# Two graph layers on one core: the first layer's result is kept in the output tensor, and the output stage's DMA adds the second layer's to it

## The chip, the cores and the metric

The kernel runs on one core of a Trainium2 chip. The core has five engines that run side by side, each with its own queue of instructions: TensorE (PE; its weight loads are listed apart as PEld), VectorE (DVE), ScalarE (ACT), GpSimd (POOL) and SyncE (SP). Data moves between the chip's memory and the on-chip SBUF through 16 DMA engines; here SP and POOL issue all transfers. TensorE writes its results to PSUM, from where VectorE or ScalarE copies them on. The metric is the time of one execution in microseconds of device time, as the median of several runs.

## What is computed

Sixteen graphs of 1024 nodes and 256 channels pass through two layers that share one adjacency matrix. The reference, cut to what matters here:

```python
# x: (16, 1024, 256), adj: (1024, 1024)
h = maximum(layernorm(x), 0)
x = x + layer0(h, para, adj, kv_w)          # attention over the nodes, weighted graph product as query
h = maximum(layernorm(x), 0)
x = x + layer1(h, adj, W1, b1, g1, be1, W2, b2, g2, be2)
return x

# layer1, in short
agg = A_hat @ h                             # A_hat: adj + I, scaled by the degrees
z   = relu(batchnorm(agg @ W1.T + b1))      # mean and variance over all graphs and nodes
y   = z @ W2.T + b2
out = batchnorm(y)                          # again over all graphs and nodes
```

Two things set the shape of the program. Each batch norm needs the statistics of all 16 graphs before any graph can go on. And the last line adds the second layer's output to `x` as it was after the first layer (called x1 here), so x1, 16 MB in all, has to be kept until the end.

## The kernel before

The batch is `B = 16`, the nodes are tiled in `NT = 8` tiles of `P = 128`, the channels in `CC = 2` chunks of 128. The function `layers` holds the first phase (layer 0, and of layer 1 everything up to `agg @ W1.T`), the function `second` holds the rest. `layers(False)` is what the profile shows. A second pass, `layers(True)`, stands behind a condition on a value that the kernel computes; no instruction of it appears in the profile. The order of the instructions on each engine is written out by hand (`tc.manual_schedule`), so what the program says in order is issued in that order.

**First phase.** Attention runs graph after graph, four scores and values steps at a time, and between these steps the generator `background(b)` supplies the other products: keys, values and queries of the next graph, the aggregate and the hidden product of the graph before. When graph b's attention is complete, `normed(b)` (line 780) takes the second layer norm of `xs[b]`, the tile that now holds x1. Then POOL stores that tile to a scratch tensor in DRAM, `x1_d[b]` (line 784; for the last graph line 795), in which each of the 128 partitions has its 8 KB in one piece. SP reloads the same SBUF tile with the input of graph b + 3 (`load_x`, line 173) and must wait for the store to have read it. Behind that load in SP's queue stand the loads of `aht`, the pieces of the combined adjacency matrix that the aggregate multiplies with (line 687, always five pieces ahead).

**Second phase, products.** `second` first runs the products `z @ W2.T` for all graphs (`graph(b, ahead)`, line 1319), reads the hidden values `yin` back from DRAM on SP's queue (line 1270), and keeps `y2[b]`, channels on partitions, in SBUF. At five places between the graphs, and before the output stage, it calls `load_x1` (line 1229). This function picks a buffer `xo` for the next graph, out of eleven in turn (three of their own, four of `yin`'s, one of `both`, and three of graphs whose `y2` is used up), and issues two loads of 512 KB from `x1_d` on SP's queue, one for each half of the nodes.

**Output stage** (from line 1430). When the statistics are complete, for each graph:

- ScalarE scales and shifts `y2[b]` in place, one instruction of 128x1024 for each of the two channel chunks (line 1437; for graph 0 four of 128x512);
- TensorE turns it, 128x128 at a time, into PSUM tiles `pt` of two node tiles each: 16 transposes in four groups of four, in four PSUM banks (line 1445);
- VectorE adds each group to its quarter of `xo` (line 1451);
- after two groups POOL stores that half, 512 KB, to `out` (line 1452), four node tiles of 1 KB rows for each partition;
- then `load_x1` fetches the next graph's x1, once its buffer is free.

The compiler gives POOL's transfers eight semaphores in turn, so a store waits until the eighth one before it has landed.

Of the kernel before, what the change touches and what calls it, by code (L numbers as in the profile page):

```python
# [10 lines left out]
F32 = mybir.dt.float32  # L11
AF = mybir.ActivationFunctionType
ALU = mybir.AluOpType
# [4 lines left out]
P = 128  # L18
# [5 lines left out]
def gnn_two_layers_kernel(  # L24
# [12 lines left out]
    nc = tc.nc  # L37
    B, N, C = x.shape
    H1 = w1_t.shape[1]
    NT = N // P  # L40
# [12 lines left out]
    dram = ctx.enter_context(tc.tile_pool(name="dram", bufs=1, space=DRAM))  # L53
# [9 lines left out]
    stats1 = const.tile([P, HC, B * NH, 6], F32, name="stats1")  # L63
    mv1 = const.tile([P, HC, 2], F32, name="mv1")

    x1_d = [dram.tile([P, NT, C], F32, name=f"x1_d{b}") for b in range(B)]


    aht_d = dram.tile([7, NP // 2, P, TH, FB], F32, name="aht_d")
# [27 lines left out]
    def layers(shifted):  # L97
# [22 lines left out]
        xs, hs, hts, ats, qs, ks, vs = {}, {}, {}, {}, {}, {}, {}  # L120
# [20 lines left out]
        def run(*parts):  # L141
            for part in parts:
                while advance(part) is not None:
                    pass
            while queue:
                queue.pop(0)()

        def weave(main, *sides):

            for i, cost in enumerate(main):  # L150
                for start, side in sides:
                    if i >= start:
                        cost += next(side, 0.0)
                yield cost
            for _, side in sides:
                yield from side
# [16 lines left out]
        def load_x(b):  # L173
            xs[b] = p3.tile([P, NT, C], F32, tag="x", name=f"x_{b}")
            for half in range(2):
                t = slice(half * NT // 2, (half + 1) * NT // 2)
                nc.sync.dma_start(
                    out=xs[b][:, t], in_=x[b].rearrange("(t p) c -> p t c", p=P)[:, t]
                )
# [205 lines left out]
        def transposed(b, k, halves=range(NH)):  # L385

            h = hs["a", b]
            if 0 in halves:
                ht = p3.tile([P, N], F32, tag="ht", name=f"ht_{b}_{k}")
                hts.setdefault(b, []).append(ht)  # L390
            ht = hts[b][k]
            for g in halves:
                pt = bank(f"htp_{b}_{k}_{g}")
                for j in range(FB // P):
                    t = g * (FB // P) + j
                    nc.tensor.transpose(
                        pt[:, j * P : (j + 1) * P], h[:, t, k * P : (k + 1) * P], ident
                    )
                nc.scalar.copy(ht[:, g * FB : (g + 1) * FB], pt)  # L399
# [351 lines left out]
        def hidden(b):  # L751
# [7 lines left out]
            for n, (g, j) in enumerate(parts):  # L759
# [17 lines left out]
                    soon(lambda: next(turns[0]))  # L777
                yield 1.71

        def normed(b):  # L780
            while (b, NH - 1) not in complete:
                yield 0.1
            yield from Norm(b, False).all()
            nc.gpsimd.dma_start(out=x1_d[b], in_=xs[b])
            if b + 3 < B:
                load_x(b + 3)

        def normed_last():

            norm = Norm(B - 1, False)  # L790
            for half in range(NH):
                while (B - 1, half) not in complete:
                    yield 0.0
                yield from norm.half(half * NT // 2)
            nc.gpsimd.dma_start(out=x1_d[B - 1], in_=xs[B - 1])

        def summed(b):
            yield from Norm(b, True).all()
# [346 lines left out]
        with st:  # L1145
            if shifted:
                for b in range(B):
                    if b > 0:
                        load_x(b)
                    run(Norm(b, True).all())  # L1150
                    differences(b)
                    for k in range(CC):
                        transposed(b, k)
                    run(islice(weighers[b], AHEAD))
                    run(weave(plain_queries(b), (0, weighers[b])))
                    if b == 0:
                        run(degrees(), graph())
                        load_later()
                    run(keys_values(b))
                    shifted_attention(b)  # L1160
                    norm = Norm(b, False)
                    run(norm.all())
                    nc.gpsimd.dma_start(out=x1_d[b], in_=xs[b])
                    if b == B - 1:
                        attn.close()
                        turns.append(second(kind))
                    run(aggregate(b), hidden(b))
            else:
                norm = Norm(0, True)
                norm.stats(0, 1)  # L1170
                norm.scale(0, 2)
                for t in range(2, NT, 2):
                    norm.stats(t, t + 1)
                    norm.shift(t - 2, 2)
                    norm.relu(t - 2, t - 1)
                    norm.scale(t, 2)
                norm.shift(NT - 2, 2)
                norm.relu(NT - 2, NT - 1)
                products = keys_values(0)

                for k in range(CC):
                    transposed(0, k, (0,))
                run(islice(products, 2))
                for k in range(CC):
                    transposed(0, k, (1,))
                differences(0)
                run(weave(products, (0, islice(weighers[0], AHEAD))))
                load_x(1)
                load_x(2)
                run(weave(plain_queries(0), (0, weighers[0]), (5, Norm(1, True).all())))  # L1190
                attention()
                attn.close()
                turns.append(second(kind))
                run(aggregate(B - 1), hidden(B - 1))
# [3 lines left out]
    def second(kind):  # L1198
# [27 lines left out]

        xos = []

        def load_x1():


            b = len(xos)
            name = f"xo_{kind}_{b}"
            HT = NT // 2
            if not 8 <= b < 11:
                pool, tag = ((xp, "xo"), (io, "yin"), (wp, "both"))[(b % 11 > 2) + (b % 11 > 6)]
                xo = pool.tile([P, NT, C], F32, tag=tag, name=name)
                halves = [xo[:, :HT, :], xo[:, HT:, :]]
            else:
                halves = [  # L1240
                    yp.tile([P, HT, C], F32, tag=f"y2_{b - 8}_{i}", name=f"{name}_{i}")
                    for i in range(2)
                ]
            for i in range(2):
                nc.sync.dma_start(out=halves[i], in_=x1_d[b][:, i * HT : (i + 1) * HT, :])
            xos.append(halves)

        with st:
# [165 lines left out]
            xp = st.enter_context(tc.tile_pool(name=f"xp_{kind}", bufs=3))  # L1414
            for b in range(B):
                graph(b, ahead_of(b + 1))
                if b in (1, 3, 5, B - 2, B - 1):
                    for _ in range(1 + b // (B - 2)):
                        load_x1()
                if kind == "f" and b == B // 2:  # L1420
                    look()
                if kind == "f" and b == B // 2 + 2:
                    flag(ps.tile([P, FB], F32, tag="pz", name=f"good_{kind}")[:, 0:1])

            scales(1)
            for _, finish, _ in affs:
                finish()
            while len(xos) < min(8, B):
                load_x1()
            for b in range(B):  # L1430

                for part in range(2 if b == 0 else 1):
                    n = slice(part * FB, N if b > 0 else (part + 1) * FB)
                    for k in range(CC):
                        s2, sh2 = affs[k][2]
                        y = y2[b][k][:, n]
                        nc.scalar.activation(y, y, AF.Identity, bias=sh2, scale=s2)
                for half in range(2):
                    xo = xos[b][half]
                    for g in range(NT // 4):  # L1440
                        pt = ps.tile([P, 2, C], F32, tag="pz", name=f"pt_{kind}_{b}_{half}_{g}")
                        for j in range(2):
                            t = half * NT // 2 + 2 * g + j
                            for k in range(CC):
                                nc.tensor.transpose(
                                    pt[:, j, k * P : (k + 1) * P],
                                    y2[b][k][:, t * P : (t + 1) * P],
                                    ident,
                                )
                        dst = xo[:, 2 * g : 2 * g + 2, :]  # L1450
                        nc.vector.tensor_add(dst, pt, dst)  # L1451
                    nc.gpsimd.dma_start(  # L1452
                        out=out[b].rearrange("(h t p) c -> h p t c", h=2, p=P)[half], in_=xo
                    )
                if len(xos) < B:
                    load_x1()

    fp = ctx.enter_context(tc.tile_pool(name="fp", bufs=1))
    bad = fp.tile([1, 1], mybir.dt.int32, name="bad")
# [16 lines left out]
    with tc.manual_schedule():  # L1476
        layers(False)
# [41 lines left out]
```

## Time and profile before

| | |
|---|---|
| median of 3 runs | 2539.81 us (2537.09 to 2540.54) |
| the profiled execution: time | 2539.22 us |
| the profiled execution: span of its instructions | 2537.4 us |
| mean granted TensorE clock | 0.986 |
| TensorE busy | 2443.6 us (96%) |
| VectorE, ScalarE, POOL busy | 74%, 55%, 17% |
| DMA traffic | 424 MB, mean 167 GB/s |
| first activation of the output stage | 2461.28 us |
| last `out` store issued | 2524.26 us |

How to read it. The span is the time from the first to the last instruction of one profiled execution, and all positions in the text are microseconds from its start. A group's line gives engine, operation, output and inputs by the program's names, shapes and count, then the busy time in all, the mean of one in ns, the idle time of the engine just before these instructions, and what ended that idle time. "L1451" is line 1451 of the kernel. The granted clock is the share of full speed that the chip's throttle let TensorE have. A DMA's landing time runs from its issue to its completion. The busy share over the whole span hides the stages: the output stage is only the last 76 us of 2537.4.

### The profile page before, as it was taken

The numbers are of one execution on the slowest core, as the hardware profiler recorded it, in microseconds if no ns is written. First come the engines' busy times: TensorE is split into PE (matmuls) and PEld (weight loads), VectorE is DVE, ScalarE is ACT, GpSimd is POOL, SyncE is SP. The second block draws the span as 40 slices with busy tenths as digits, with TensorE's granted clock in tenths as the row PEclk, the third lists the DMA queues.
The fourth block names the chain that finished last, engine by engine and source line by source line (L and its number), as shares of the span: only waits on it lengthen the run. The fifth ranks groups of instructions, "written<-read, shape, count | busy, mean of one in ns | idle before, by whom it ended". The sixth has DMA issues, their size and how long they took to land. (4 is left out here: it accounts for less than half of the span.)

```text
span 2537.4 us, 35520 instructions
## 1 busy us (share of the span) xinstructions
PE 2443.6 (96%) x13343; PEld 833.1 (33%) x13343; DVE 1886.3 (74%) x2924; ACT 1399.2 (55%) x1919; POOL 428.8 (17%) x532
## 2 busy tenths in 40 slices
PE   8979999999999999999999999999999999999994
PEld 3323333333333333333333333333333332234443
DVE  4658787777878687878777787868786866656774
ACT  6756464747474655646474747465565634345553
POOL 1460101010101101010101010110101001036653
PEclk9989999999999999999999999999999999999997
DMA  4663535444454535352544444443535244355459
GB/s 141 202 213 97 218 97 198 136 178 162 170 166 146 183 131 181 102 204 89 207 131 177 159 170 166 172 157 133 184 112 195 84 154 160 131 216 216 182 200 363
DMA packets 189108, 424.03 MB, mean 167 GB/s; under 512 B 22200, under 2 KB 84672, under 8 KB 181120
## 3 DMA queue, kind: packets, MB, share of 16 engines
q1 hardware_dynamic: 161408, 312.87, 36.4%
q0 software_dynamic: 27520, 108.81, 11.3%
q8 instruction: 107, 1.75, 0.3%
q14 instruction: 73, 0.60, 0.1%
HBM read 316.94 MB, written 104.66 MB: 166 GB/s over the span
## 5 line engine op out<-in xcount | busy, mean ns | idle before, releaser
L931 ACT ACTIVATE p<-sc 128x1024 f32<-128x1024 f32 x512 | 495.0, 1019 | 637.0 <-PE sc L923 636.6
L953 DVE TENSOR_TENSOR acc<-acc,p 128x1024 f32<-128x1024 f32 x384 | 470.9, 1226 | 172.4 <-ACT p L931 151.8
L923 PE MATMUL sc<-q,k 64*64 64x512 f32 x4096 | 503.3, 607 | 8.8 <-ACT p L931 8.8
L964 PE MATMUL o<-p,v 128*64 128x512 f32 x2048 | 497.2, 606 | 2.2 <-DVE os L978 2.2
L171 PE MATMUL pg<-w,h_a 128*64 128x512 f32 x1600 | 359.8, 592 | 0.9 <-DVE w L467 0.9
L171 PE MATMUL pa<-aht,h_b 128*64 128x512 f32 x1536 | 347.4, 594 | 5.5 <-DMA aht<-aht_d 4.9
L480 ACT ACTIVATE w<-cbc,csum 128x512 f32<-128x512 f32 x256 | 285.8, 1168 | 0.0
L923 PEld LDWEIGHTS sc<-q,k 64*64 64x64 f32 x4096 | 132.0, 133 | 354.1 <-issue 300.9
L467 DVE SCALAR_TENSOR_TENSOR w<-w,adj 128x1024 f32<-128x1024 f32 x128 | 156.3, 1221 | 111.6 <-ACT w L488 91.5
L171 PE MATMUL py<-at,w 128*64 128x512 f32 x1024 | 229.2, 594 | 0.0
L982 POOL DMA_DIRECT2D out_d<-os x63 | 35.6, 565 | 1126.7 <-DVE os L978 1121.4
L964 PEld LDWEIGHTS o<-p,v 128*64 128x64 f32 x2048 | 125.2, 137 | 305.2 <-issue 274.4
L171 PEld LDWEIGHTS pg<-w,h_a 128*64 128x64 f32 x1600 | 114.8, 137 | 229.1 <-issue 219.2
L171 PEld LDWEIGHTS pa<-aht,h_b 128*64 128x64 f32 x1536 | 110.3, 137 | 220.0 <-issue 201.8
L767 ACT ACTIVATE y<-py,vec 128x512 f32<-128x512 f32 x128 | 87.4, 683 | 120.6 <-PE py L171 97.0
L488 ACT ACTIVATE w<-w 128x1024 f32<-128x1024 f32 x128 | 135.1, 1056 | 1.7
L542 DVE TENSOR_TENSOR w<-w,w 128x1024 f32<-128x1024 f32 x112 | 132.7, 1215 | 1.5
L768 POOL DMA_DIRECT2D y_d<-y x128 | 69.3, 541 | 350.3 <-ACT y L767 345.5
L171 PEld LDWEIGHTS py<-at,w 128*64 128x64 f32 x1024 | 74.4, 138 | 146.1 <-issue 133.3
L171 PE MATMUL pk<-ht,kvw_f 128*64 128x512 f32 x512 | 117.6, 603 | 1.5 <-ACT ht L399 1.5
L171 PE MATMUL pv<-kvw_f,ht 128*64 128x256 f32 x1024 | 116.1, 379 | 0.0
L950 DVE TENSOR_TENSOR acc<-p,p 128x1024 f32<-128x1024 f32 x64 | 78.7, 1230 | 49.8 <-ACT p L931 49.7
(163 smaller groups left out, 2639.2 us busy)
## 6 DMA issues: line engine op xcount, KB each, us to landing
aht<-aht_d SPq DMA_DIRECT2D x224, 512.0 KB, 6.5
adj<-in_adj_dram SPq DMA_DIRECT2D x128, 512.0 KB, 4.7
y_d<-y POOLq DMA_DIRECT2D x128, 256.0 KB, 4.0
yin_f<-y_d SPq DMA_DIRECT2D x32, 1024.0 KB, 6.4
x<-in_x_dram SPq DMA_DIRECT2D x32, 512.0 KB, 5.3
para<-in_para_dram SPq DMA_DIRECT2D x64, 256.0 KB, 3.1
x_d<-x POOLq DMA_DIRECT2D x16, 1024.0 KB, 9.9
xo_f<-x_d SPq DMA_DIRECT2D x32, 512.0 KB, 8.1
```

The lines of the kernel that those rows point to most:

```text
L171: nc.tensor.matmul(dst[r], left[:, r], right, start=start, stop=stop)
L467: nc.vector.scalar_tensor_tensor(w, w, 1.0, a, op0=ALU.add, op1=ALU.mult)
L480: nc.scalar.activation(w[:, t, :].rearrange("p (t q) -> p t q", q=P), cbc[:, q * NT // NH : (q + 1) * NT // NH], AF.Abs, bias=csum[:, th * ...
L488: nc.scalar.activation(made[i], made[i], AF.Tanh, scale=-0.5 / C)
L542: nc.vector.tensor_sub(block(i)[part], block(x)[part], block(y)[part])
L767: nc.scalar.activation(y, made, AF.Identity, bias=b1[:, j : j + 1])
L768: nc.gpsimd.dma_start(out=y1_d[i][:, j, :], in_=y)
L923: nc.tensor.matmul(sc[part, e, :], ks[b][k][r, m * P + c * HW : m * P + (c + 1) * HW], qs[b][k][r, f * FB : (f + 1) * FB], start=True, sto ...
L931: nc.scalar.activation(pr, sc, AF.Exp)
L950: nc.vector.tensor_add(self.acc, self.held, pr)
L953: nc.vector.tensor_add(self.acc, self.acc, pr)
L964: nc.tensor.matmul(self.o[r, :], vs[b][k][:, m, r], pr[:, e, :], start=(m == 0), stop=(m == NT - 1),)
```

## The change

x1 is no longer stored to `x1_d`, which goes away. A new function `keep(b)` stores it to `out[b]`, in the output's layout. It is called where the stores to `x1_d` stood. `load_x1` becomes `output_tile`: it picks the same buffers in the same turn, but loads nothing, and is called once for each graph at the start of its turn in the output stage. Three quarters of a graph's result are copied from PSUM by VectorE, the last one by ScalarE. POOL's store adds to what stands in `out` (`accum_op=ALU.add`).

```diff
-    x1_d = [dram.tile([P, NT, C], F32, name=f"x1_d{b}") for b in range(B)]
...
+        def keep(b):
+
+            nc.gpsimd.dma_start(out=out[b].rearrange("(t p) c -> p t c", p=P), in_=xs[b])
+
         def normed(b):
             while (b, NH - 1) not in complete:
                 yield 0.1
             yield from Norm(b, False).all()
-            nc.gpsimd.dma_start(out=x1_d[b], in_=xs[b])
+            keep(b)
             if b + 3 < B:
                 load_x(b + 3)
...
-            nc.gpsimd.dma_start(out=x1_d[B - 1], in_=xs[B - 1])
+            keep(B - 1)
...
-        def load_x1():
+        def output_tile():
...
-            for i in range(2):
-                nc.sync.dma_start(out=halves[i], in_=x1_d[b][:, i * HT : (i + 1) * HT, :])
             xos.append(halves)
...
             for b in range(B):
                 graph(b, ahead_of(b + 1))
-                if b in (1, 3, 5, B - 2, B - 1):
-                    for _ in range(1 + b // (B - 2)):
-                        load_x1()
...
-            while len(xos) < min(8, B):
-                load_x1()
             for b in range(B):
 
+                output_tile()
                 for part in range(2 if b == 0 else 1):
...
                         dst = xo[:, 2 * g : 2 * g + 2, :]
-                        nc.vector.tensor_add(dst, pt, dst)
+                        if half + g < 2:
+                            nc.vector.tensor_copy(dst, pt)
+                        else:
+                            nc.scalar.copy(dst, pt)
                     nc.gpsimd.dma_start(
-                        out=out[b].rearrange("(h t p) c -> h p t c", h=2, p=P)[half], in_=xo
-                    )
-                if len(xos) < B:
-                    load_x1()
+                        out=out[b].rearrange("(h t p) c -> h p t c", h=2, p=P)[half],
+                        in_=xo,
+                        accum_op=ALU.add,
+                    )
```

More of the change, by code (lines that the diff above doesn't have):

```diff
@@ L1162, in layers @@
                     run(norm.all())
-                    nc.gpsimd.dma_start(out=x1_d[b], in_=xs[b])
+                    keep(b)
                     if b == B - 1:
```

## The prediction

> **What bounds the kernel now.** I read the busy time by stage first, then the groups of the output stage, its first microseconds in order of time, the granted clock, and last the chain of waits and the DMA issues.
>
> Busy time by stage (start:end, length, then busy time and count of PE, PEld, DVE, ACT, POOL, granted clock, DMA share, GB/s):
>
> ```profile
> 2287.00:2442.00 155.00, 155.00 (x364) 68.67 (x363) 107.33 (x161) 84.01 (x117) 98.80 (x39) 1.00 0.52 196
> 2442.00:2461.00 19.00, 14.98 (x35) 6.28 (x33) 15.13 (x24) 0.86 (x2) 9.31 (x7) 1.00 0.62 203
> 2466.00:2511.00 45.00, 37.68 (x244) 28.13 (x242) 36.93 (x61) 32.65 (x29) 17.38 (x23) 0.88 0.98 388
> 2511.00:2537.40 26.40, 0.00 (x0) 0.00 (x0) 1.02 (x2) 0.00 (x0) 6.76 (x9) 0.50 0.85 297
> ```
>
> Until 2442 TensorE is busy all the time (155 of 155 us), and the reloads of the first layer's result that run there cost nothing. From 2466 the bound is the DMA engines (0.98 busy); after 2511 only stores are left. So what the change is worth is read from 2461 to the end.
>
> The groups of that stage (busy, mean ns, idle before):
>
> ```profile
> L1445 PE MATMUL pt_f<-ident,y_f 128*128 128x128 f32 x256 | 40.9, 307 | 10.5 <-ACT y_f L1437 5.8 <-DVE xo_f L1451 3.2 <-ACTq L1480 1.2
> L1451 DVE TENSOR_TENSOR xo_f<-pt_f,xo_f 128x512 f32<-128x512 f32 x64 | 39.4, 682 | 10.2 <-SPq L1480 3.7 <-DMA xo_f<-x_d 3.6 <-PE pt_f L1445 2.9
> L1437 ACT ACTIVATE y_f<-y_f,sm_f 128x1024 f32<-128x1024 f32 x30 | 34.1, 1228 | 0.0
> L1452 POOL DMA_DIRECT2D out_dram<-xo_f x32 | 24.1, 756 | 39.0 <-DMA out_dram<-xo_f 20.1 <-DVE xo_f L1451 13.6 <-DMA xo_f<-x_d 5.3
> ```
>
> ScalarE's 30 long activations have no idle time before them: it only scales `y`, waits for nobody and runs ahead (34.1/30 = 1.14 us apart, each 1.23 long). TensorE and VectorE follow at about 2.4 us a graph.
>
> The chain of waits and the issues of the stage:
>
> ```profile
> 2510.16 10.37 DMA out_dram<-xo_f
> 2523.53 0.72 POOL out_dram L1452
> out_dram<-xo_f POOLq DMA_DIRECT2D x32, 512.0 KB, 12.5
> xo_f<-x_d SPq DMA_DIRECT2D x16, 512.0 KB, 12.3
> ```
>
> The end is set by stores: a store may be issued only when the eighth before it has landed.
>
> **The change part by part.** *Reloads removed.* All 32 loads leave SP's queue; 16 of them (8.4 MB) lie behind 2461, where the engines are full. At the 410 GB/s of 2471 to 2511 that is 8.4/0.410 = 20 us of DMA time. The other 16 were hidden by TensorE; the `yin` loads behind them on SP come earlier, which a full TensorE turns into nothing.
>
> *VectorE's 64 adds (682 ns) become 48 copies.* It no longer waits for loads. A copy from PSUM on VectorE is not in the trace; between the 424 ns of its SBUF copy of 128x512 and the 682 of the add, three take 1.3 to 2.0 us a graph, beside the transposes, so nothing.
>
> *ScalarE gets 16 copies: the term that decides.* In the compiled order of its queue the copy of graph b's last quarter stands between the activations of b and those of b+1. It waits for the last transposes of b, which wait for b's own activations. Behind it in the queue are the activations of b+1, and for these TensorE waits. What ran side by side becomes a ring: activations, 16 transposes, copy, and only then the next graph. Its pieces come from the first graph, where the transposes also follow at once:
>
> ```profile
> 2461.28 0.81 ACT L1437 ACTIVATE y_f<-y_f,sm_f 128x512 f32<-128x512 f32 x1 [13.82 <-DVE sm_f L1216]
> ...
> 2463.29 6.88 PE L1445 MATMUL pt_f<-ident,y_f 128*128 128x128 f32 x35 [0.67 <-ACT y_f L1437]
> 2464.24 0.69 DVE L1451 TENSOR_TENSOR xo_f<-pt_f,xo_f 128x512 f32<-128x512 f32 x1 [1.84 <-PE pt_f L1445]
> 2465.09 0.69 DVE L1451 TENSOR_TENSOR xo_f<-pt_f,xo_f 128x512 f32<-128x512 f32 x1 [0.16 <-PE pt_f L1445]
> ...
> 2466.79 0.69 DVE L1451 TENSOR_TENSOR xo_f<-pt_f,xo_f 128x512 f32<-128x512 f32 x1 [0.16 <-PE pt_f L1445]
> ```
>
> Groups of four transposes end 0.85 us apart, 0.21 each, and VectorE starts 0.53 after the last of a group was issued (2463.29 + 2 x 0.21 = 2463.71; start 2464.24). The same by granted clock:
>
> ```profile
> 2465.00:2468.00 3.00, 3.00 (x15) 2.60 (x14) 2.16 (x4) 3.00 (x4) 1.07 (x2) 0.50 0.21 44
> 2471.00:2474.00 3.00, 2.97 (x23) 2.20 (x22) 3.00 (x6) 3.00 (x4) 2.11 (x3) 1.00 1.03 400
> 2504.00:2507.00 3.00, 2.53 (x11) 2.12 (x12) 1.74 (x3) 0.00 (x0) 0.75 (x1) 0.50 1.03 415
> ```
>
> At 0.50 a transpose takes 0.21; at 1.00 the weight loads of eight run back to back in 0.95 us, 0.12 each. One turn of the ring: the second activation ends at 1.14 + 1.23 = 2.37; a semaphore 0.06 (2463.23 to 2463.29); one transpose has been done after the first activation, of the other 15 the last is issued 14 steps on; the copy starts 0.53 later (0.4 at full clock) and takes this:
>
> ```profile
> L399 ACT COPY ht<-htp x12: 563/587/612, 12.6 to 180.1; 128x512 f32<-128x512 f32 x12
> ```
>
> At half clock: 2.37 + 0.06 + 14 x 0.21 + 0.53 + 0.59 = 6.5 us. At full clock: 2.37 + 0.06 + 14 x 0.12 + 0.4 + 0.59 = 5.1 us. I take 6.45 (and 5.05 below: an activation starts some 0.05 before the copy ahead of it ends): after 2501 TensorE worked in bursts of eight with gaps of 1.2 to 1.4 us and fell from 1.00 to 0.50; the ring leaves it idle for about 3 us in 6.5, and it enters the stage at 0.50.
>
> [...]
>
> *The stores accumulate.* No row shows one. Below: no more than a plain store, 333 GB/s (2521 to 2531), which is 16.78/0.333 = 50 us for all. Above: the destination's bytes are read as well, so as much as a load and a store. At 410 GB/s for both that is 205 GB/s of result; at twice the stores-only time 166. The ring asks for 1.05 MB in 6.45 us, 163 GB/s. So up to this price the ring still decides, and I add nothing but the last landing: a plain store lands in 5.6 us at best and I take 8, between once and twice that. The queue's limit of eight allows worse; that is the second rival. On POOL an issue takes 0.756; at double, 1.5, two fit in 6.45.
>
> [...]
>
> *The first layer's result goes to the output's place:* 16 stores of 1 MB in rows of 1 KB instead of 8. POOL's issue, 0.62 now, is at most 2 x 0.756 = 1.5; POOL's next instruction in the turn at 384.83 comes 15.5 us later, so nothing. SP waits for it before it may reload `x`:
>
> ```profile
> SPq L177 <- DMA x_d<-x: 104.8, 13, 10.0
> PE pa L171 <- DMA aht<-aht_d: 4.9, 1, 4.9
> ```
>
> Behind that wait stand the `aht` loads, and here the cover is thin: in the turn at 384.83 five pieces were ahead, the sixth was issued at 395.55 and its products begin at 401.4, while such a load lands in 6.5 us at the median. How much later may the store land? There it shared the engines with five pieces, 3.67 MB in 9.7 us, 378 GB/s. Below: rows of 1 KB ran beside loads at 410 (after 2471), so not later at all; above: 1.05/0.333 = 3.1 us for itself, all of it on top. I take 0, the row nearest to a mixture; above it costs 13 x 3 = 39 us.
>
> **The sum.** The first graph's last copy starts at 2466.79 as now, ends 2467.38. 15 turns: 15 x 6.45 = 96.8, so 2564.1. Issue 0.64 (2509.53 to 2510.16), landing 8, and 0.6 to the end of the span (the last stores, issued 2524.26, landed after 10.3 to 12.8): 2573.4. Against the span of 2537.4 that is +36.0. The profiled execution took 2539.22, so 2575.2; the median shown is 0.6 higher, within the scatter, and I predict 2575. The full-clock ring gives 2467.38 + 15 x 5.05 + 9.24 = 2552.4, or 2554 us. With the best landing it is 2552.
>
> **Rivals.**
> (1) *Full-clock ring*, 2554 us. For it: 2469 to 2497 at 1.00 on transposes alone. Against: that took gapless work. Counted with the forecast.
> (2) *The accumulating stores bound.* Eight in flight landed in 21.1 us at worst, when loads and stores shared the engines. If the read before each write doubles that, 42.2 us for 8 x 0.524 = 4.19 MB is 99 GB/s: 16.78/0.099 = 169 us from 2466.1, span about 2636, 2638 us. It decides from below 163 GB/s. For it: DMA was the bound already. Against: 20 us of loads are gone.
> (3) *Faster.* ScalarE's copy does not hold up the next activations (or the ring is under (2537.4 - 9.24 - 2467.38)/15 = 4.05 us a turn). Then ScalarE needs 2 x 1.14 + 0.59 = 2.9 us a graph, ends near 2509, and stores at the plain rate end at 2466.1 + 50.4 + 3 = 2520: 2522 us. For it: the DMA bound it removes is real. Against: the queue's order, and transposes would have to be at 0.05 us.
> (4) *Late `aht` pieces in the first layer*, up to 39 us on top, 2614 us. For it: the thin cover. Against: the 410 GB/s of the mixture.
>
> **How the numbers follow.** Ring, either clock: 0.61 (half clock 0.48). Stores bound: 0.26. Late pieces: 0.06. Faster: 0.04; a mixture near no change 0.03. A measurement of this kernel tells about 0.2% (5 us) from no change. So faster 0.04, same 0.03, slower 0.93. Range: from the full-clock ring, 2550, to rival (2), 2640; the ring's own is 2552 to 2582.
>
> **What would show it.** The ring: ScalarE's activations get idle time ended by TensorE's transposes, and pairs start 6 to 6.5 us apart; the granted clock reads near 0.5 from 2470. Rival (2): POOL's waits for its own stores grow far beyond 20.1 us, DMA is full to the end, and ScalarE or VectorE ends long before. The first layer is right if the first activation of the stage still starts near 2461. I am wrong if turns are under 4.05 us, or if an accumulating 512 KB lands alone in far more than 11 us.

## The result and the profile after

| | before | after |
|---|---|---|
| median | 2540.18 us (2537.09 to 2542.82, 4 runs) | 2575.79 us (2575.3 to 2578.32, 4 runs) |
| ratio to before | | 1.0146, 95% interval 1.0133 to 1.0159 |
| profiled execution: time / span | 2539.22 / 2537.4 us | 2578.32 / 2576.4 us |
| mean granted TensorE clock | 0.986 | 0.976 |
| DMA traffic of the span | 424 MB | 407 MB |
| first activation of the output stage | 2461.28 us | 2464.26 us |
| last `out` store, start of its issue | 2524.24 us | 2564.99 us |

The change makes the kernel 35.6 us slower, although the profile counts 17 MB less traffic. (That is the reloads: 300.16 MB read from the chip's memory instead of 316.94, and 104.66 MB written in both. From 2461 on the profile counts 16.90 MB with accumulating stores, in e1 below, and the same 16.90 with plain ones, in e3. So a read of the destination isn't in this count, and whether the memory is really read less is open.) One execution of all those in this document was far off: one of the four of e1, below, took 3684.93 us at a granted clock of 0.653, and e1's ratio leaves it out. Busy time by stage of the kernel after (start:end, length, then busy time and count of PE, PEld, DVE, ACT, POOL, granted clock, DMA share, GB/s):

```profile
2442.00:2461.00 19.00, 17.96 (x42) 7.60 (x40) 13.97 (x21) 4.28 (x7) 10.48 (x4) 1.00 0.00 0
2466.00:2511.00 45.00, 27.06 (x115) 22.55 (x116) 14.52 (x21) 21.61 (x24) 18.09 (x14) 0.58 1.04 146
2511.00:2560.00 49.00, 28.99 (x127) 23.90 (x125) 16.41 (x24) 22.47 (x24) 20.51 (x16) 0.60 1.19 168
2560.00:2576.40 16.40, 3.46 (x15) 3.06 (x15) 2.07 (x3) 0.95 (x2) 2.59 (x3) 0.50 0.87 128
```

The reloads are gone from 2442 to 2461 (0 GB/s, where 203 stood). In the 45 us after 2466 only 115 transposes are recorded where 244 stood before, and the transposes go on to the end. From 2466 on no engine is busy for much more than 60% of a stretch, and the clock reads 0.5 to 0.6: that is the picture of a chain of waits, not of a full engine. The DMA share of 1.04 to 1.19 looks like a full resource, and a later run shows that it isn't.

The groups of the stage (busy, mean ns, idle before and what ended it):

```profile
L1442 PE MATMUL pt_f<-ident,y_f 128*128 128x128 f32 x256 | 60.0, 413 | 43.9 <-ACT y_f L1434 43.9
L1452 POOL DMA_DIRECT2D out_dram<-xo_f x32 | 41.2, 1287 | 60.3 <-DVE xo_f L1449 54.5 <-ACT xo_f L1451 4.9 <-issue 0.7
L1434 ACT ACTIVATE y_f<-y_f,sm_f 128x1024 f32<-128x1024 f32 x30 | 35.6, 1235 | 0.0
L1449 DVE COPY xo_f<-pt_f 128x512 f32<-128x512 f32 x48 | 33.0, 691 | 65.4 <-PE pt_f L1442 64.9
L1451 ACT COPY xo_f<-pt_f 128x512 f32<-128x512 f32 x16 | 9.4, 586 | 53.5 <-PE pt_f L1442 43.4 <-issue 10.1
```

ScalarE's copies waited 43.4 us for TensorE's transposes, and TensorE's transposes waited 43.9 us for ScalarE's activations. Two engines that wait for each other for the same 44 us take turns. The activations show no idle time of their own because the copy in front of them in the queue has taken it. POOL never waits for its own stores any more (20.1 us before).

One turn in order of time (start, duration, what, and the idle time before it):

```profile
2482.09 0.59 ACT L1451 COPY xo_f<-pt_f 128x512 f32<-128x512 f32 x1 [3.55 <-PE pt_f L1442]
2482.58 2.37 ACT L1434 ACTIVATE y_f<-y_f,sm_f 128x1024 f32<-128x1024 f32 x2
...
2483.87 0.48 PE L1442 MATMUL pt_f<-ident,y_f 128*128 128x128 f32 x1 [1.81 <-ACT y_f L1434]
2485.00 3.46 PE L1442 MATMUL pt_f<-ident,y_f 128*128 128x128 f32 x15 [0.65 <-ACT y_f L1434]
...
2488.55 0.59 ACT L1451 COPY xo_f<-pt_f 128x512 f32<-128x512 f32 x1 [3.61 <-PE pt_f L1442]
```

Copy, two activations, sixteen transposes, copy: 6.46 us from copy to copy. The first copy starts at 2469.77, the last at 2563.96: 15 turns of 6.28 us in the mean.

The end of the chain of waits, and the DMA issues (count, KB of each, median us to landing):

```profile
2560.42 2.62 PE pt_f L1442 x11
...
2566.03 0.24 POOL out_dram L1452
out_dram<-x POOLq DMA_DIRECT2D x16, 1024.0 KB, 11.0
out_dram<-xo_f POOLq DMA_DIRECT2D x32, 512.0 KB, 7.1
```

Before, the chain came through `DMA out_dram<-xo_f`. Now it comes through the transposes, and an accumulating store lands after 7.1 us at the median, where a plain one among reloads took 12.5.

### The profile page after: what moved, and what is told of

It reads as the page before. It is cut to its first block, busy times and chain, and to the rows that moved or that the text cites. A ratio compares the mean times of both kernels' runs of the same rounds, so it can differ in the third digit from the quotient of the medians.

```text
span 2576.4 us, 35475 instructions
## 1 busy us (share of the span) xinstructions
PE 2460.6 (96%) x13343; PEld 850.8 (33%) x13343; DVE 1877.7 (73%) x2908; ACT 1409.2 (55%) x1935; POOL 451.5 (18%) x532
## 3 DMA queue, kind: packets, MB, share of 16 engines
q0 software_dynamic: 41856, 108.81, 13.9%
HBM read 300.16 MB, written 104.66 MB: 157 GB/s over the span
```

## The experiments

Ten kernels. "Before" in their ratios is the kernel before, run beside them on the same chip (medians of 2538.99 to 2539.87 us). e2 and e7 are one run each.

| run | what it is | median | ratio to before |
|---|---|---|---|
| e1 | all copies on VectorE, accumulating stores | 2561.85 us | 1.0082 [1.0062, 1.0102] |
| e2 | ring, plain stores | 2573.92 us, one run | |
| e3 | all copies on VectorE, plain stores | 2528.42 us | 0.9951 [0.9934, 0.9967] |
| e4 | activations ahead of the copy, accumulating | 2559.62 us | 1.0077 [1.006, 1.0094] |
| e5 | e4 with runs of 4 KB | 2557.61 us | 1.0078 [1.0062, 1.0093] |
| e6 | before with runs of 4 KB | 2538.07 us | 0.9995 [0.9986, 1.0004] |
| e7 | e2 with TensorE kept busy | 2549.74 us, one run | |
| e8 | the change for graphs 8 to 15 only | 2546.26 us | 1.0031 [1.0019, 1.0043] |
| e9 | the change for odd graphs only, two queues | 2547.24 us | 1.0036 [1.0022, 1.005] |
| e10 | after with TensorE kept busy | 2561.91 us | 1.0091 [1.0074, 1.0108] |

### The two suspects, one at a time

The theory was the ring; the rival was the price of the accumulating stores. Four kernels take away one, the other, both, or break the ring in another way.

e1, all four copies on VectorE:

```diff
-                        if half + g < 2:
-                            nc.vector.tensor_copy(dst, pt)
-                        else:
-                            nc.scalar.copy(dst, pt)
+                        nc.vector.tensor_copy(dst, pt)
```

> All four quarters are copied by VectorE, so that ScalarE's queue holds only activations; stores accumulate as in the changed kernel. Theory ring (the copy in ScalarE's queue sets the pace, the DMA engines have room): VectorE goes at about 2.5 us a graph and ends near 2508, the stores then go at up to 205 GB/s or more, 2522 to 2558 us. Theory DMA (at 163 GB/s the accumulating stores were as good as full, DMA share 1.04 to 1.19, and the ring only happened to have the same pace): 2570 to 2580 us, landings grow from 7 us to over 20, POOL waits for its own stores.

e2, the ring as it is, the store plain (it leaves out the addition of the first layer's result):

```diff
                         in_=xo,
-                        accum_op=ALU.add,
                     )
```

> The changed kernel with a plain store in place of the accumulating one; it leaves out the addition of the first layer's result (the output is the second layer's part alone). Theory ring: ScalarE's copies stay 6.3 us apart, the last one lands some 2 us sooner, 2572 to 2577 us. Theory DMA: turns get shorter than 6.0 us, or the end comes more than 5 us sooner.

e3, both edits (it leaves out the same addition):

> VectorE copies everything and the store is plain; it leaves out the addition of the first layer's result. Both theories: neither the ring nor the read before the write is left, so plain stores at 333 GB/s bind: 16.78/0.333 = 50 us from about 2468, 2520 to 2528 us. The difference of e1 to this run is the price of accumulating once the ring is gone.

e4, the ring broken in ScalarE's queue instead, with the copy left on ScalarE (cut: `scaled(b)` is a new function that holds the two activations of graph b; it is called for graph 0 ahead of the loop, and no longer at the start of each turn):

```diff
                         else:
+                            if b + 1 < B:
+                                scaled(b + 1)
                             nc.scalar.copy(dst, pt)
```

> The changed kernel, except that in ScalarE's queue the activations of graph b+1 stand before the copy of graph b's last quarter. Theory ring: the ring is open, ScalarE needs 2 x 1.14 + 0.59 = 2.9 us a graph, and the time falls to that of e1 within 4 us. Theory DMA: stays at 2570 to 2580 us.

Without the ring the time falls by 14 us (e1) and 16 us (e4), whichever way the ring is broken, but not to the time of before. e1's 2561.9 us lies between the ranges of the two theories: the ring was holding the time, as the first has it, but the accumulating stores cost more than its 205 GB/s allowed, and the second's signs, landings over 20 us and POOL's waits, are there too. In e4 ScalarE has no idle time left, and its copies are 2.74 us apart:

```profile
2476.95 0.57 ACT L1458 COPY xo_f<-pt_f 128x512 f32<-128x512 f32 x1
2477.41 2.38 ACT L1433 ACTIVATE y_f<-y_f,sm_f 128x1024 f32<-128x1024 f32 x2
2479.69 0.57 ACT L1458 COPY xo_f<-pt_f 128x512 f32<-128x512 f32 x1
```

What stands in the way then is read from the stages, the waits and the issues of e1:

```profile
2466.00:2511.00 45.00, 37.30 (x250) 27.82 (x248) 38.30 (x64) 33.89 (x30) 28.60 (x22) 0.92 1.14 178
2511.00:2540.00 29.00, 0.00 (x0) 0.00 (x0) 0.00 (x0) 0.00 (x0) 12.85 (x10) 0.50 1.24 198
...
POOL out_dram L1449 <- DMA out_dram<-xo_f: 17.3, 12, 1.8
...
out_dram<-xo_f POOLq DMA_DIRECT2D x32, 512.0 KB, 20.7
```

The compute is done by 2511, as it was before the change. After that only accumulating stores run, at a steady 198 GB/s with landings of 20.7 us at the median, for some 45 us more. POOL's wait for its own stores, gone in the kernel after, is back. And 198 GB/s at a DMA share of 1.24 is what full looks like here: the kernel after, at 146 to 168 GB/s, was not full.

The same stretch in e2 and in e3, with their store landings:

```profile
2466.00:2511.00 45.00, 26.81 (x116) 22.43 (x117) 14.51 (x21) 21.71 (x24) 10.63 (x14) 0.61 0.47 160
out_dram<-xo_f POOLq DMA_DIRECT2D x32, 512.0 KB, 3.4
```

```profile
2466.00:2511.00 45.00, 34.58 (x245) 26.15 (x243) 37.35 (x62) 32.76 (x29) 23.00 (x31) 0.92 0.94 306
out_dram<-xo_f POOLq DMA_DIRECT2D x32, 512.0 KB, 11.4
```

In e2 the stores are nearly idle (share 0.47, landing after 3.4 us), and the stage is as slow as in the kernel after: 116 transposes in 45 us, 6.23 us a turn in the mean. So the ring alone is enough to make the time. In e3, with neither, the kernel would be 11.5 us faster than before (0.4 us above the upper end of the expected range): with these copies and these rows of 1 KB, this is what the removed reloads could have brought.

Put one after the other, the parts are: the reloads gone, -11.5 us (e3 against before); accumulating instead of plain stores, +33.4 (e1 against e3); the ring, +13.9 (after against e1). That they add up to the slowdown proves nothing, since each step starts where the one ahead of it ends. In the other order the ring would be charged with 45.5 (e2 against e3) and accumulating with 1.9 (after against e2). Two limits stand close to each other, 6.28 us a graph for the ring and 1.05/0.198 = 5.3 for the stores, and taking either away alone shows only the distance to the other.

### Is the price of accumulating one of the small packets?

A trace of the stage shows another difference: accumulating stores move in packets of 1 KB (e1: 16896 packets for 16.78 MB), POOL's plain ones in packets of 4 KB (e3: 4608 packets for 16.78 MB). e5 is e4 with the nodes laid out so that each partition's half graph is one run of 4 KB:

```diff
-                                    y2[b][k][:, t * P : (t + 1) * P],
+                                    y2[b][k].rearrange("p (q t) -> p t q", t=NT)[:, t],
...
-                        out=out[b].rearrange("(h t p) c -> h p t c", h=2, p=P)[half],
+                        out=out[b].rearrange("(p h t) c -> h p t c", h=2, p=P)[half],
```

> The scale-ahead kernel (2559.6 us, accumulating stores at 198 GB/s in packets of 1 KB), with the nodes of the output stage laid out so that each partition's half of a graph is one contiguous run of 4 KB of the output instead of four runs of 1 KB; the transposes read the second layer's result at a stride of 8 nodes for it. Theory that an accumulated byte has its price whatever its run: packets larger or not, 190 to 205 GB/s in the middle of the stage, landings near 20 us, 2556 to 2563 us. Rival, that the price is one of the 1 KB packets: above 240 GB/s, landings below 12 us, 2525 to 2545 us. A third reading, that a column read at a stride of 8 slows the transposes: over 413 ns of one at the full clock and a time above 2563 us.

The DMA queue of the stage (queue: packets, MB, share), first of e10 below, which accumulates in 1 KB rows, then of e5, and e5's rate when only stores are left:

```profile
q0 software_dynamic: 16118, 16.02, 121.9%
```

```profile
q0 software_dynamic: 4608, 16.78, 92.0%
2511.00:2540.00 29.00, 0.00 (x0) 0.00 (x0) 0.00 (x0) 0.00 (x0) 7.76 (x9) 0.53 1.07 211
```

The packets are four times as large, and the rate goes from 198 to 211 GB/s. That is past the 205 of the first theory and far from the 240 of the rival. The longer run is worth some 6% of the rate, and in the time 2 us, which the intervals of e4 and e5 don't tell apart. So the price is not one of the small packets. (The strided transposes cost nothing that shows: 293 ns of one in the stage, 291 in e4.)

e6 gives the kernel before the same layout, and with it the 1 KB rows of the first-layer store that the changed kernel has:

> The kernel before, with the first layer's result kept in an internal tensor in the output's order (stored in rows of 1 KB in the first phase, as the changed kernel does), and reloaded and added and stored in runs of 4 KB in the output stage, the transposes at a stride of 8 nodes. If the 1 KB rows of the first-layer store cost nothing in the first phase, as the changed kernel's trace suggested, and run length doesn't matter to plain transfers from 1 KB up: 2537 to 2543 us, no change. If longer runs make the stage's stores quicker: the stage moves 25.2 MB at up to 410 GB/s, and a twentieth of that is 3 us: 2530 to 2537 us. If the strided read slows the transposes: above 2545 us.

0.9995, interval 0.9986 to 1.0004: the longer runs and the first-layer store in 1 KB rows together don't move the time. Its trace shows more than that. The last stretch in which only plain stores are left:

```profile
2516.00:2521.00 5.00, 0.00 (x0) 0.00 (x0) 0.00 (x0) 0.00 (x0) 2.13 (x4) 0.50 1.03 415
```

Plain stores alone ran at 333 GB/s in the kernel before (2521 to 2526) and ran at 415 here, with runs of 4 KB. It shows so little in the time because stores are alone only in the last 15 us. Now plain and accumulating stores can be compared at the same run length: 333 against 198 GB/s in rows of 1 KB, 415 against 211 in runs of 4 KB, where accumulating carries 0.59 and 0.51 of the plain rate. A read of the destination ahead of each write was my supposition; no run shows one.

### Is it TensorE's clock that holds the turn?

e7 is e2 (so the addition is left out again) with transposes of the identity, whose result nobody uses, in TensorE's gap:

```diff
+                        if half == g == 0:
+                            for _ in range(22):
+                                nc.tensor.transpose(pt[:, 0, 0:P], ident, ident)
```

> The changed kernel with a plain store (the addition of the first layer's result is left out, as in the run with the ring and a plain store, 2573.9 us and 6.4 us a turn), and 22 transposes of the identity onto itself in front of each graph's first group, in TensorE's gap of 3.5 us, so that TensorE is never idle for long. Theory that the turn's length is set by 14 transposes at half clock (0.21 us each): granted clock above 0.9 in the stage, transposes near 0.11 us, turns of 5.0 to 5.6 us, 2552 to 2562 us. Rival, that the clock isn't what holds the turn: turns of 6.3 us or more, 2572 us or above.

One stretch of the kernel after, and the same of e7:

```profile
2474.00:2500.00 26.00, 16.07 (x67) 13.30 (x66) 8.62 (x13) 11.42 (x12) 10.29 (x8) 0.50 1.17 166
```

```profile
2474.00:2500.00 26.00, 23.71 (x210) 22.53 (x209) 10.98 (x18) 14.53 (x16) 7.83 (x11) 1.00 0.66 223
```

(TensorE's gaps in a turn of the kernel after are 1.81 and 0.65 us; the 3.5 us of the expectation is nearer to ScalarE's wait, 3.55.) A turn of e7 in order of time:

```profile
2480.49 0.59 ACT L1454 COPY xo_f<-pt_f 128x512 f32<-128x512 f32 x1 [2.00 <-PE pt_f L1445]
...
2480.97 2.37 ACT L1434 ACTIVATE y_f<-y_f,sm_f 128x1024 f32<-128x1024 f32 x2
...
2483.40 1.86 PE L1445 MATMUL pt_f<-ident,y_f 128*128 128x128 f32 x15 [0.49 <-ACT y_f L1434]
...
2485.29 0.59 ACT L1454 COPY xo_f<-pt_f 128x512 f32<-128x512 f32 x1 [1.95 <-PE pt_f L1445]
```

Three times as many instructions on TensorE, and the kernel is 24 us faster than e2. The same 15 transposes take 1.86 us instead of 3.46, the granted clock reads 1.00 instead of 0.50, and the turn takes 4.80 us instead of 6.46. In the mean of its 15 turns it is 4.87 us, shorter than the 5.0 expected, and the time lies 2 us below the expected range. The clock theory holds.

e10 puts the same filler into the changed kernel itself, accumulating stores and all:

> The changed kernel itself, accumulating stores and ring kept, with the 22 transposes of the identity in TensorE's gap ahead of each graph. By its own turn the ring would now take 4.8 us a graph (as with plain stores, 2549.7 us), which asks for 1.05 MB per 4.8 us, 218 GB/s. Theory that accumulating stores carry at most 198 GB/s (5.3 us a graph): the stores bind, landings grow towards 20 us, and the time is that of the kernels without the ring, 2557 to 2564 us, not 2550. Rival, that the 198 GB/s were due to many stores in flight at once and that a paced queue does better: landings stay below 10 us, 2550 to 2555 us.

```profile
2511.00:2540.00 29.00, 23.69 (x205) 22.28 (x205) 11.31 (x18) 14.87 (x16) 15.58 (x12) 1.00 1.24 198
out_dram<-xo_f POOLq DMA_DIRECT2D x32, 512.0 KB, 12.0
```

The ring now turns in 4.83 us in the mean, and the time is that of the kernels without the ring, 2561.9 us. The stores take 198 GB/s whether a ring paces them or eight wait in flight. Their landings grow from 6.4 to 16.8 us through the stage (12.0 at the median): the backlog that 4.83 us of work against 5.3 us of transfer piles up. I had expected them nearer to 20; the ring is a smaller step ahead of the stores than the kernels without it.

### Would the change pay where the reloads weren't hidden?

Half of the reloads were hidden behind TensorE before the stage, and the other half ran inside it. e8 makes the change only for graphs 8 to 15, whose reloads ran inside it, with all copies on VectorE (the edit against the kernel before, cut; the first-layer stores of these graphs go to `out` too):

```diff
-            for i in range(2):
+            for i in range(2 if b < 8 else 0):
                 nc.sync.dma_start(out=halves[i], in_=x1_d[b][:, i * HT : (i + 1) * HT, :])
...
-                        nc.vector.tensor_add(dst, pt, dst)
+                        if b < 8:
+                            nc.vector.tensor_add(dst, pt, dst)
+                        else:
+                            nc.vector.tensor_copy(dst, pt)
...
+                        accum_op=ALU.bypass if b < 8 else ALU.add,
```

> The change made for half of the graphs. Graphs 0 to 7, whose reloads lie ahead of the stage, are as before (reload, addition on VectorE, plain store); graphs 8 to 15, whose reloads ran in the stage, have their first layer's result in the output, copies on VectorE and accumulating stores. Theory that an accumulated MB costs 1/198 of a ms and that the reload it replaces is worth as much: 8.4 MB plain at 330 to 410 GB/s is 20 to 25 us, 8.4 MB accumulated at 198 is 42 us, from 2466 that ends at 2528 to 2533, and with the last landing and the 2 us around the span 2533 to 2543 us, no change within 0.2%. Rival, that accumulating has a cost of its own beyond its bytes (the change loses whichever graphs it is made for): above 2546 us.

e9 makes it for the odd graphs, and lets SyncE issue the plain stores (the edit against the kernel after, cut to the stores; the even graphs are reloaded and added as before):

```diff
-                    nc.gpsimd.dma_start(
-                        out=out[b].rearrange("(h t p) c -> h p t c", h=2, p=P)[half],
-                        in_=xo,
-                        accum_op=ALU.add,
-                    )
+                    to = out[b].rearrange("(h t p) c -> h p t c", h=2, p=P)[half]
+                    if b % 2 == 0:
+                        nc.sync.dma_start(out=to, in_=xo)
+                    else:
+                        nc.gpsimd.dma_start(out=to, in_=xo, accum_op=ALU.add)
```

> As the run before it, but the even graphs are as before and the odd ones accumulate, and the plain stores are issued by SyncE, so that plain and accumulating stores run side by side on two queues. Theory that both draw on the same transfer engines: the sum is the same 63 to 68 us, 2532 to 2543 us. Rival, that accumulating waits for something that plain stores don't use (the engines idle meanwhile): the stage is then bound by the larger of the two, 42 us of accumulating stores or 45 us of VectorE, and ends near 2511 to 2515, 2515 to 2525 us, faster than the kernel before.

Stages of e8, then of e9:

```profile
2475.00:2480.00 5.00, 4.94 (x36) 3.46 (x33) 5.00 (x10) 5.00 (x6) 3.23 (x5) 1.00 1.01 317
...
2490.00:2495.00 5.00, 4.93 (x36) 3.46 (x33) 5.00 (x10) 5.00 (x5) 3.73 (x3) 1.00 1.05 247
...
2511.00:2525.00 14.00, 0.00 (x0) 0.00 (x0) 0.00 (x0) 0.00 (x0) 5.13 (x4) 0.50 1.24 198
```

```profile
2511.00:2525.00 14.00, 0.00 (x0) 0.00 (x0) 0.00 (x0) 0.00 (x0) 0.00 (x0) 0.50 1.18 239
```

Both are 0.3% slower than before, past both of the "no change" ranges. The term I had wrong is the plain half: I counted 330 to 410 GB/s, and plain stores alone ran at 312 to 317 (2475 to 2490; behind that the accumulating ones join in), because the 388 GB/s of the kernel before was reloads and stores together. 8.4 MB at 0.315 is 27 us, plus 42 at 198 GB/s: 69 us from 2466, where the kernel before moves 25.2 MB in 61 to 65. e8 alone doesn't separate this from the rival, at whose border (2546) it stands. e9 speaks for shared engines: 16.8 MB at 239 GB/s take 70 us, nearly the same sum, though two kinds of store run side by side on two queues. (SyncE's plain stores moved in packets of 1 KB here, 8302 for 8.24 MB, so that e9 differs from e8 in this too.) If accumulating had left the engines free for others, e9 would have ended near 2520. No version here beats the kernel before; e6 equals it. Runs of 4 KB would at best have brought e8 level with e6, by an estimate from the rates of e5 and e6: 8.4 MB at 415 and 8.4 MB at 211 GB/s are 60 us, and e6 moves its 25.2 MB at 416 GB/s (2471 to 2511) in 61.

## Why the prediction was right

The forecast of 2575 us was the ring's, and the ring made the time. Point by point:

- *Reloads removed, 20 us of DMA time.* They left the stage, and the engines were no longer the bound, as said. What this brings without the ring and the accumulating is smaller: 11.5 us (e3), because the remaining plain stores ran at 306 to 330 GB/s and not at the 410 of the mixture. The forecast's sum didn't use this number.
- *VectorE's copies, 0.42 to 0.68 us each, hidden.* They took 0.69, as long as the adds (691 ns against 682). In the kernel after VectorE is idle for 65 us before them.
- *The ring, 6.45 us a turn.* Eight of the 15 turns took 6.40 to 6.46, the other seven 5.8 to 6.3 with some transposes at a higher clock (0.58 to 0.60 in the stage's long stretches). The mean of 6.28 made 94.2 us of the 96.8 forecast, 2.6 less.
- *The clock.* I argued from gaps of 1.2 to 1.4 us that had cost it before. In a turn of the kernel after TensorE is idle for 1.81 to 1.87 and about 0.65 us, 2.5 in all where I wrote about 3, and in two pieces, since one transpose follows the first activation; the clock was at half for most of the stage all the same. It did come back for some microseconds at a time, and fell again:

```profile
2470.00:2473.00 3.00, 0.65 (x4) 0.47 (x5) 0.00 (x0) 2.63 (x3) 1.75 (x2) 1.00 0.74 87
```

  From 2474 it reads 0.50 again. It fell with no gap above 1.87 us, and in e7 it read 1.00 from 2474 to 2500 with gaps of 0.43 to 0.49.
- *The accumulating stores, 166 to 205 GB/s, so not the bound.* 198 measured. The ring asked for 1.05/6.28 = 167, so it decided, with 0.98 us a graph to spare. The read of the destination from which I worked out the range was my supposition, and no run shows one; what the runs show is 198 GB/s for accumulating stores and 306 to 330 for plain ones (e1, e3).
- *POOL's issue, 0.756 to 1.5.* 1.28, twice in 6.28 us: no bound. The last issue starts 0.44 us after the last copy, where I had 0.64.
- *The last landing, 8 us.* 9.1, counted from the start of the issue as in the forecast: 1.1 too little.
- *The end of the span, 0.6 us behind it.* 2.3, so 1.7 too little, and this was a misreading of the trace before: the last store there lands after 10.9 us, not 12.8, at 2535.1, so that 2.3 us lie behind the last landing in both kernels.
- *The first-layer store in 1 KB rows, 0 where up to 39 were possible.* It takes 0.97 us to issue (1.5 was the bound), and lands after 11.0 us instead of 9.9. SyncE waits longer for it; TensorE's waits don't grow. From the waits of the kernel after (total, times, longest):

```profile
SPq L176 <- DMA out_dram<-x: 128.1, 13, 10.8
...
PE pa L170 <- ACT h_b L340: 4.9, 2, 4.3
```

  SyncE's wait grew from 104.8 to 128.1 us, while TensorE's listed waits ahead of the aggregate's products went from 5.5 us (4.9 of them put down to `aht`) to 4.9. The store lands later, and the cover was enough. e6, with the same store, doesn't move.
- *The start of the stage.* I took it as unchanged; the profiled execution starts it 2.98 us later. In e1 to e5, e7 and e10, which share the whole program up to there with it, the first activation stands anywhere from 2459.3 to 2464.4, so this is scatter between executions. The three other executions of the kernel after had spans of 2573.8, 2573.2 and 2573.8, about the forecast's 2573.4.
- *The sum.* +3.0 at the start, -2.6 in the turns, -0.2 at the issue, +1.1 at the landing and +1.7 behind it make the +3.0 between the span forecast and 2576.4. Without the start they cancel: the mechanism was right, and that the median came within 1 us of the forecast is partly luck.

The rivals. The *full-clock ring* (1) did not occur, and its 2554 was priced wrong: at 5.05 us a turn the ring asks for 208 GB/s, above the 198 of the stores, so that they bind, and e10 took 2561.9. *Stores bound* (2) had the mechanism that stands right behind the ring, with the rate taken at half of what it is (99 GB/s); at 198 it lies above the 163 from which it would have decided. *Faster* (3) needed both the ring and the price of accumulating to be absent: e3 is that case, 2528.4 where I wrote 2522. *Late `aht` pieces* (4) did not occur.

## What to carry to other kernels

The DMA that adds saved a load and an instruction's operand, but not transfer time: 1 MB added took 5.3 us, and 1 MB loaded and 1 MB stored took 5.1 at the 410 GB/s of the stage before. So it took work off the load queue and added the price of the loads that had been hidden. When a step is moved to another engine, read what stands behind it in that engine's queue: a copy that waits for this round's result, ahead of the work for the next round, made a ring here out of engines that had run side by side, and the sign of it in the profile was two engines that waited for each other for the same time. And after a bound is found, ask how far behind it the next one stands: the ring cost 45 us or 14, by what was left beside it.

## What the runs showed that I had not expected

- POOL's accumulating stores move in packets of 1 KB where its plain stores of the same shape move in 4 KB (16896 and 4608 packets for 16.78 MB in e1 and e3; SyncE's plain stores, in e9, move in 1 KB as well, 8302 for 8.24 MB). Runs of 4 KB raised the accumulating ones only from 198 to 211 GB/s, and plain stores alone from 333 to 415.
- A DMA share above 1 doesn't say that the engines are full: the kernel after shows 1.19 at 168 GB/s, and the same stores reach 198 at 1.24.
- An accumulating store takes POOL 1.28 us to issue, a plain one 0.756. With runs of 4 KB it was 0.87 (e5) and 0.54 (e6).
- TensorE's clock was at half from 2474 to 2500 with no gap longer than 1.87 us and a busy share of 62% (16.07 of 26 us). In e4, with gaps of 0.78 us and 72% (18.64 of 26 us), it read 1.00. Filling the gaps with useless work made the turns of the changed kernel's ring 1.45 us shorter in the mean (6.28 to 4.83).
